# A gated recurrent layer on one core: half B's first memory scan put ahead of half A's second update, and the x products cut into other pieces

## The chip, the cores and the metric

The kernel runs on one core of a Trainium2 chip. The core has a matrix engine (TensorE, PE in the profile; its weight loads are listed apart as PEld), a vector engine (VectorE, DVE), a scalar engine (ScalarE, ACT), a general engine (GpSimd, POOL) and a queue engine (SyncE, SP) that issues DMAs. They run side by side and wait for each other through semaphores. Each of VectorE, ScalarE and GpSimd works through its instructions in the order in which the program lists them. The metric is device time in microseconds of one execution.

## The reference

The layer runs over 512 time steps, for 8 sequences (batch) and 512 hidden units, and its result is added to the input:

```python
def step(h, x_t):
    fused = sigmoid(concatenate([x_t, h]) @ w_W + w_b)
    hidden_state, output_state = split(fused, 2)          # r and z
    memory_state = x_t @ wx_W + wx_b + hidden_state * (h @ wh_W + wh_b)
    h_new = output_state * h + (1.0 - output_state) * tanh(memory_state)
    return h_new
x + all h_new
```

All is in float32. The products with `x_t` depend on nothing that the loop makes; the products with `h` must wait for the previous step's `h_new`.

## The kernel before

**Layout.** The 512 hidden units are four chunks of 128. Chunks 0 and 1 of the state are half A (`hTA`), chunks 2 and 3 half B (`hTB`), each [128 partitions, 8 batch columns, 2 chunks, 3 slots]. A product uses one chunk of state as weights (32 columns) and streams a weight matrix; four of them (j = 0 to 3) write the four 32-partition strips of the output at once. "A group of four" below is such a quadruple.

**One step on TensorE** (line 27, `ORDER`). A0 A1 take the two chunks of `hTA` against 256 columns each, A2 A3 the two chunks of `hTB` against 192 columns each, all into the PSUM tile A; D0 to D3 take all four chunks against 128 columns into tile D; H2 H3 take `hTB` against 64 columns into tile H. Then comes a piece of the products with x for steps to come (line 393), and the next step's A0.

**One step on VectorE** (lines 470 to 495). For half A: transpose `tr` (r gate), transpose into `md1A` (the h product), transpose `tz` (z gate), a one-column memset of the tile `idle`, two memory scans `m` (one for each chunk). Then, for half B: a transpose of a part of A into `md1B` (line 452), `tr` from D, the first update scan of A, the transpose of H into `md1B`, `tz` from D, the second update scan of A, two memory scans, two update scans of B. The memory scan computes r * (h product) + x part, and the update scan z * h + (1 - z) * tanh. ScalarE computes the sigmoids of `tr` (into `md0`) and of `tz` (into `hd0`), the tanh behind each memory scan (into a slot of `hTA` or `hTB`), and a copy of the new state.

The one-column memsets compute nothing. The one at line 441 carries a wait: it waits for VectorE's own transpose into `md1A`, so that the memory scan behind it has to wait for ScalarE's sigmoid alone. For half B the same is reached in another way: the second update of A is made to wait for B's sigmoid (line 481), and the first memory scan of B behind it waits for VectorE's own transpose. Two more memsets stand at the end of every step (line 569).

**Who waits for whom.** A0 needs the first update of A, A1 the second, A2 the first update of B, A3 the second. `tr` of half A needs A3 done, `tr` of half B needs D, the transpose into `md1B` needs H.

**The products with x** (lines 296 to 342). They are made for eight steps (two groups of four steps) at a time, by seven products instead of eight: `x_sum` (GpSimd) and `weight_sum` (VectorE) form sums of x columns and of weights; p1 and p7, p2 and p6, p4 and p3 are run in pairs (j = 0, 1 from the first, j = 2, 3 from the second), and `shared` is added into both banks `xps`. Each k is one half of a contraction. `products` yields after each piece, and the main loop takes one piece per step, from step 4 of eight on. The pieces are 384, 384, 384, 384 columns in steps 4 to 7 of eight, and 288, 96 + 192, 192 + 96, 288 in steps 0 to 3. Around them ScalarE fills the banks with bias (line 534) and copies finished ones to `xs`, VectorE adds the shared differences (lines 508 to 548), and the `x_sum` of the first kind used (number 2) is issued in step 3 of eight (line 539). Nothing is planned by a tool: the order on each engine is the order of the statements.

Of the kernel before, what the change touches and what calls it, by code (L numbers as in the profile page):

```python
# [19 lines left out]


DVE_FILL = 23
IDLE = 3
LAST = 4
SYNC = mybir.DependencyInfo(mybir.DependencyClass.Sync, mybir.DependencyReason.DATA)

# [22 lines left out]
def tile_cond_rnn_residual(  # L49
# [39 lines left out]
    nc = tc.nc  # L89
# [27 lines left out]
    def x_of(c, k, t, n):  # L117

        e, t = divmod(t, TC // 2)
        if c == 0 and e == 0:  # L120
            first = head[:, :NX].rearrange("p (k n) -> p k n", k=NQ)
            return first[:, k, t * B : (t + n) * B]
        return xins[c][:, e, k, t * B : (t + n) * B]
# [19 lines left out]
    def pair(n, name, rows, slots):  # L143

        return const.tile([P, 2, rows, slots], F32, name=name).rearrange("p c n s -> p n c s")
# [24 lines left out]
    for t_ in hd0[0] + hd0[1]:  # L170
        nc.gpsimd.memset(t_[:, :, :, 1], -1.0)
    idle = const.tile([P, IDLE], F32, name="idle")

# [8 lines left out]
    def state(hf, i, slot=2):  # L182

        s = i % GS
        return hT[hf][i % NH][:, B * s : B * s + B, :, slot]
# [8 lines left out]
    def mm(out_, lhsT, rhs, start=False):  # L194
        nc.tensor.matmul(  # L195
            out_, lhsT, rhs, start=start, stop=False, skip_group_check=True
        )
# [27 lines left out]
    def act(key, out_, in_, func, **kw):  # L225
        inst = nc.scalar.activation(out_, in_, func, **kw).ins  # L226
        if key in written:
            tc.declare_no_dep(inst, written[key], reason="ordered through VectorE")
        written[key] = inst
        return inst  # L230

    def seed(g):

        nc.scalar.copy(xps[g % 2][:, COLS], bias[:, COLS])
# [32 lines left out]
    def wx_of(kh, nh):  # L267
        return wx[:, 2 * kh : 2 * kh + 2, 2 * nh : 2 * nh + 2]

    def x_half(o, n, kh):  # L270

        return x_of(o // 2, slice(2 * kh, 2 * kh + 2), 8 * (o % 2) + GS * n, GS)
# [12 lines left out]
    def x_sum(o, n):  # L285

        t_ = [q[o % 2] for q in sx]
        a, b, op = [
            (x_half(o, 1, 0), x_half(o, 1, 1), ALU.add),
            (t_[0], x_half(o, 0, 0), ALU.subtract),  # L290
            (x_half(o, 0, 0), x_half(o, 1, 0), ALU.subtract),
            (x_half(o, 0, 1), t_[1], ALU.subtract),
        ][n]
        nc.gpsimd.tensor_tensor(t_[n], a, b, op)

    def products(o):

        t_ = [q[o % 2] for q in sx]
        p1 = (0, x_half(o, 0, 0), wx_of(0, 0))
        p2 = (0, x_half(o, 0, 1), wx_of(1, 0))  # L300
        p3 = (0, t_[3], wx_of(1, 1))
        p4 = (1, x_half(o, 1, 1), tw[3])
        p6 = (0, t_[1], tw[1])
        p7 = (1, t_[2], tw[2])

        def pair(left, right, k, c0=0, c1=WIDE):
            for j in range(NQ):
                bank, lhs, rhs = left if j < 2 else right
                mm(
                    xps[bank][32 * j : 32 * j + 32, COLS.start + c0 : COLS.start + c1],  # L310
                    lhs[:, k],
                    rhs[:, k, j % 2, c0:c1],
                    start=right is p7 and k == 0 and j >= 2,
                )

        def shared(k):
            for j in range(NQ):
                c0 = HALF * (1 - j // 2)
                mm(
                    xps[j // 2][32 * j : 32 * j + 32, COLS.start : COLS.start + HALF],  # L320
                    t_[0][:, k],
                    tw[0][:, k, j % 2, c0 : c0 + HALF],
                )

        pair(p1, p7, 0)
        yield
        pair(p1, p7, 1)
        yield
        pair(p2, p6, 0)
        yield  # L330
        pair(p2, p6, 1)
        yield
        pair(p4, p3, 0, 0, 288)
        yield
        pair(p4, p3, 0, 288)
        shared(0)
        yield
        shared(1)
        pair(p4, p3, 1, 0, 96)
        yield  # L340
        pair(p4, p3, 1, 96)
        yield

    def take(it, n=None):
        while n is None or n > 0:
# [20 lines left out]
    for i in range(T):  # L366
# [8 lines left out]
        for n in (ORDER if i else FIRST).split():  # L375
# [3 lines left out]
            bank, k = n[0], int(n[1])  # L379
# [17 lines left out]
        def scan(c_, out_, d0, d1):  # L397

            return nc.vector.tensor_tensor_scan(  # L399
                *[t_[:, :, c_].rearrange("p n c s -> p (n c s)") for t_ in (out_, d0, d1)],  # L400
                0.0,
                ALU.mult,
                ALU.add,
            ).ins
# [8 lines left out]
        def turned(n, hf):  # L413
            t_ = work.tile([P, 2, 32], F32, tag=f"t{n}{hf}", name=f"t{n}{hf}_{i}")
            inst = nc.vector.transpose(t_.rearrange("p c n -> p (c n)"), raw[n][hf]).ins  # L415
            return t_[:, :, rows], inst

        r_done = [None, None]
        h_done = [None, None]
# [17 lines left out]

        def turn_z(hf):
            tz, _ = turned("z", hf)
            if hf == 0:  # L440
                inst = nc.vector.memset(idle[:, IDLE - 1 :], 0.0).ins
                tc.add_manual_dep(inst, h_done[0].name, SYNC)
            act(
                ("zc", hf, i % 2),
                hd0[hf][i % 2][:, :, :, 2].rearrange("p n c -> p c n"),
                tz,
                AF.Sigmoid,
                scale=-1.0,
            )
# [9 lines left out]
        def memory(hf, q):  # L459

            c_ = slice(q, q + 1)
            scan(c_, ms[hf], md0[hf][g % 2][:, rows], md1[hf][g % 2][:, rows])
            act(("n", hf, q, i % NH), state(hf, i, 1)[:, :, c_], ms[hf][:, :, c_, 1 + hf], AF.Tanh)

        def update(hf, q):
            s1 = (i + 1) % GS
            new = hT[hf][(i + 1) % NH][:, B * s1 : B * s1 + B]
            return scan(slice(q, q + 1), new, hd0[hf][i % 2], hT[hf][i % NH][:, rows])
# [9 lines left out]
        update(0, 0)  # L478
        turn_h(1)
        turn_z(1)  # L480
        tc.add_manual_dep(update(0, 1), r_done[1].name, SYNC)
        if i == 0:

            seed(2)
        if i == T - 1:
            nc.gpsimd.tensor_tensor(
                ot[:, t, :2, :].rearrange("p c n -> p n c"),
                x_of(c, slice(0, 2), t, 1).rearrange("p c n -> p n c"),
                state(0, T),
                ALU.add,  # L490
            )
        memory(1, 0)
        memory(1, 1)
        update(1, 0)
        update(1, 1)
# [5 lines left out]
        o, u = divmod(i, 2 * GS)  # L501
        nxt, two = o + 1 < NG // 2, o + 2 < NG // 2
# [15 lines left out]
        if u == 0:  # L518
            spread(2 * o + 1, "D")
            if o and nxt:  # L520
                nc.scalar.copy(xps[0][Q01, lo], step_bias[Q01])
                nc.scalar.copy(xps[1][Q23, lo], step_bias[Q23])
        elif u == 1:
            spread(2 * o + 1, "A")
            if o == 0:
                seed(3)
        elif u == 2:
            if o == 0:
                nc.scalar.copy(xs[0][:, SC], xps[0][:, COLS])
            elif nxt:  # L530
                nc.scalar.copy(both[Q23, HALF:], xps[0][Q01, lo])
                nc.vector.tensor_copy(both[Q23, :HALF], xps[1][Q23, lo])
            if two:
                nc.scalar.copy(xps[0][Q01, COLS], bias[Q01, COLS])
        elif u == 3:
            if o == 0:
                nc.scalar.copy(xs[1][:, SC], xps[1][:, COLS])
            if two:
                x_sum(o + 2, 2)
        elif u == 4 and nxt:  # L540
            if o:
                add_(xs[1][Q01, SC], xps[1][Q01, COLS], u3[Q23], ALU.add)
            spread(2 * o + 2, "A")
            if two:
                x_sum(o + 2, 0)
        elif u == 5 and nxt:
            if o:
                add_(xs[1][Q23, SC], u3[Q23], both[Q23], ALU.add)
            if two:
                nc.scalar.copy(xps[0][Q23, COLS], xps[0][Q01, COLS])  # L550
                x_sum(o + 2, 1)
            spread(2 * o + 2, "D")
        elif u == 6 and nxt:
            spread(2 * o + 2, "H")
            if two:
                nc.vector.memset(xps[1][Q01, COLS], 0.0)
                x_sum(o + 2, 3)
        elif u == 7 and nxt:
            if two:
                nc.scalar.copy(u2[Q23], xps[0][Q23, COLS])  # L560
            spread(2 * o + 3, "H")
# [4 lines left out]
        if i == 4:  # L566
            for to, c_ in ((Q01, slice(256, 448)), (Q23, slice(64, 256))):
                nc.vector.tensor_tensor(step_bias[to], bias[Q23, c_], bias[Q01, c_], ALU.subtract)
        for n in range(IDLE - 1):
            nc.vector.memset(idle[:, n : n + 1], 0.0)  # L570
        def add(hf, engine):
            return engine.tensor_tensor(  # L572
# [98 lines left out]
```

## Time and profile before

| | |
|---|---|
| median of 3 runs | 1681.23 us (1681.18 to 1681.54) |
| profiled execution, its own time | 1681.52 us |
| its span in the profile | 1679.7 us |
| TensorE busy | 1667.8 us, 99% |
| VectorE busy | 1402.8 us, 84% |
| ScalarE busy | 1190.5 us, 71% |
| GpSimd busy | 327.2 us, 19% |
| granted TensorE clock | 1.00 |

The span is what lies between the first and the last instruction of the profiled execution. In a row of the timeline stand start, duration, engine, line, operation, the tiles written and read, and how many neighbouring instructions were merged (x16); a bracket gives the idle time before it and who ended it. A row of the groups gives busy time, mean duration in ns, and idle time before it with what ended it. A matmul's record lasts until its result is out and so overlaps the next one's: the distance between starts tells the pace, not the duration. Each float32 product appears as two records.

### The profile page before, as it was taken

How to read it: one execution, taken by the hardware profiler on the slowest of the kernel's cores; microseconds unless marked ns; L12 is line 12 of the kernel's file. 1: busy time of each engine (PE TensorE's matmuls, PEld its weight loads, DVE VectorE, ACT ScalarE, POOL GpSimd, SP SyncE). 2: the span in 40 equal slices, each digit the busy share in tenths (PEclk: the TensorE clock that was granted, in tenths of full speed). 3: DMA queues.
4: the chain of work that ended last, by engine and by line, in shares of the span. 5: the costliest groups of instructions: out<-in, count | busy, mean ns of one | idle time of the engine just before them, and what ended most of it. 6: DMA issues, size and time to landing. Idle time of an engine off the chain costs nothing.

```text
span 1679.7 us, 110201 instructions
## 1 busy us (share of the span) xinstructions
PE 1667.8 (99%) x46078; PEld 1237.3 (74%) x46078; DVE 1402.8 (84%) x10213; ACT 1190.5 (71%) x5884; POOL 327.2 (19%) x1290
## 2 busy tenths in 40 slices
PE   8999999999999999999999999999999999999998
PEld 5777777777777777777777777777777777777776
DVE  6888888888888888888888888888888888888886
ACT  4777777777777777777777777777777777777775
POOL 2221121111211211112112121121121211211211
PEclk9999999999999999999999999999999999999999
DMA  4000000000000000000000000000000000000000
GB/s 178 17 4 17 17 17 17 12 9 17 17 17 17 4 17 17 17 17 4 17 17 17 17 16 5 17 17 17 17 4 17 17 17 17 4 17 11 11 11 10
DMA packets 11452, 30.14 MB, mean 18 GB/s; under 512 B 1220, under 2 KB 1732, under 8 KB 10952
## 3 DMA queue, kind: packets, MB, share of 16 engines
q1 hardware_dynamic: 10800, 22.94, 3.9%
q8 instruction: 360, 5.90, 1.5%
q14 instruction: 140, 1.15, 0.2%
q10 hardware_dynamic: 152, 0.16, 0.0%
HBM read 14.70 MB, written 8.39 MB: 14 GB/s over the span
## 4 chain that ended last, share of the span: by engine, by line
PE 97%; DVE 2%; DMA 1%; ACT 0%; issue 0%
PE A L195 48%; PE D L195 26%; PE xp L195 17%; PE H L195 7%; DMA wd<-in_wd_dram 1%; DVE tr L415 0%; DMA rows<-in_bias_dram 0%; DVE m L399 0%; DVE md1B L452 0%; DVE tw L283 0%; DVE tz L415 0%; DVE md1A L431 0%; DVE hTA L399 0%; DVE hTB L399 0%; ACT hTB L226 0%
## 5 line engine op out<-in xcount | busy, mean ns | idle before, releaser
L195 PE MATMUL A<-wa,hTA 128*32 128x256 f32 x8176 | 535.3, 379 | 3.0 <-DVE hTA L399 3.0
L195 PE MATMUL A<-wa,hTB 128*32 128x192 f32 x8176 | 436.2, 331 | 0.0
L195 PEld LDWEIGHTS A<-wa,hTA 128*32 128x32 f32 x8176 | 255.6, 122 | 233.0 <-DVE hTA L399 171.3
L572 POOL TENSOR_TENSOR ot<-xin,hTB 128x16 f32<-128x16 f32 x503 | 124.8, 248 | 1312.0 <-DVE hTB L399 1301.0
L195 PEld LDWEIGHTS A<-wa,hTB 128*32 128x32 f32 x8176 | 250.8, 123 | 165.8 <-DVE hTB L399 145.4
L195 PE MATMUL D<-wd,hTA 128*32 128x128 f32 x8192 | 317.6, 273 | 1.2 <-DMA wd<-in_wd_dram 1.2
L195 PE MATMUL D<-wd,hTB 128*32 128x128 f32 x8192 | 317.5, 273 | 0.0
L226 ACT ACTIVATE md0A<-tr 128x16 f32<-128x16 f32 x512 | 112.8, 220 | 231.0 <-DVE tr L415 221.6
L195 PEld LDWEIGHTS D<-wd,hTA 128*32 128x32 f32 x8192 | 257.2, 122 | 22.2 <-DMA wd<-in_wd_dram 1.5
L195 PE MATMUL xp<-tw,sx 128*32 128x384 f32 x1984 | 265.3, 406 | 0.0
L415 DVE STREAM_TRANSPOSE tr<-A 128x64 f32<-128x64 f32 x511 | 127.9, 250 | 137.0 <-PE A L195 127.7
L195 PEld LDWEIGHTS D<-wd,hTB 128*32 128x32 f32 x8192 | 240.4, 122 | 0.0
L399 DVE TENSOR_TENSOR_SCAN hTB<-hd0B,hTB 128x24 f32<-128x24 f32 x1024 | 159.9, 198 | 94.4 <-ACT hTB L226 94.4
L195 PE MATMUL H<-wa,hTB 128*32 128x64 f32 x8192 | 208.2, 219 | 0.0
L195 PE MATMUL xp<-wx,xin 128*32 128x384 f32 x1056 | 207.9, 486 | 0.0
L399 DVE TENSOR_TENSOR_SCAN hTA<-hd0A,hTA 128x24 f32<-128x24 f32 x1024 | 194.8, 190 | 0.0
L195 PEld LDWEIGHTS H<-wa,hTB 128*32 128x32 f32 x8192 | 185.5, 122 | 0.0
L226 ACT ACTIVATE hTB<-hTB 128x16 f32<-128x16 f32 x512 | 121.3, 237 | 78.4 <-DVE hTB L399 66.2
L226 ACT ACTIVATE hd0B<-tz 128x16 f32<-128x16 f32 x512 | 115.7, 226 | 74.9 <-DVE tz L415 27.6
L226 ACT ACTIVATE hTB<-m 128x8 f32<-128x8 f32 x1024 | 163.8, 208 | 4.4
L226 ACT ACTIVATE hTA<-m 128x8 f32<-128x8 f32 x1024 | 160.5, 206 | 2.2
L399 DVE TENSOR_TENSOR_SCAN m<-md0A,md1A 128x16 f32<-128x16 f32 x1024 | 142.2, 181 | 8.8
(103 smaller groups left out, 2586.2 us busy)
## 6 DMA issues: line engine op xcount, KB each, us to landing
xin<-in_x_dram SPq DMA_DIRECT2D x31, 256.0 KB, 3.5
out_dram<-ot SPq DMA_DIRECT2D x31, 256.0 KB, 2.1
wx<-in_wx_dram SPq DMA_DIRECT2D x4, 768.0 KB, 6.8
wa<-in_wa_dram SPq DMA_DIRECT2D x4, 512.0 KB, 9.6
wd<-in_wd_dram SPq DMA_DIRECT2D x1, 768.0 KB
wd<-in_wd_dram SPq DMA_DIRECT2D x1, 256.0 KB, 11.2
out_dram<-ot SPq DMA_DIRECT2D x1, 192.0 KB, 1.9
head<-in_xh_dram ACTq DMA_DIRECT2D x1, 144.0 KB, 4.8
```

Source lines behind the costliest of these rows:

```text
L195: nc.tensor.matmul(out_, lhsT, rhs, start=start, stop=False, skip_group_check=True)
L226: inst = nc.scalar.activation(out_, in_, func, **kw).ins
L399: return nc.vector.tensor_tensor_scan(*[t_[:, :, c_].rearrange("p n c s -> p (n c s)") for t_ in (out_, d0, d1)], 0.0, ALU.mult, ALU.add,).ins
L415: inst = nc.vector.transpose(t_.rearrange("p c n -> p (c n)"), raw[n][hf]).ins
L572: return engine.tensor_tensor(ot[:, t, 2 * hf : 2 * hf + 2, :].rearrange("p c n -> p n c"), x_of(c, slice(2 * hf, 2 * hf + 2), t, 1).rearr ...
```

## The change

Three things are changed together. On VectorE the first memory scan of half B comes ahead of the second update of half A; that update no longer waits for B's sigmoid, and half B gets a one-column memset of its own that waits for the transpose of H, as half A has. The pieces of the x products become 128 (only for the first of eight steps of a later set; it is taken at the end of the step before), 256 + 64, 320, 384, 384, 320, 64 + 192 + 64, 192 + 128, 192 columns, so that six steps of eight have 320 and two have 384. Since the first piece of the next set now runs at the end of step 3 of eight, its `x_sum` is issued in step 2, and the start flag is set only on the piece that begins at column 0. The number of one-column memsets at the end of a step stays two; `seed(2)` of the first step moves by one statement.

```diff
--- before.py
+++ after.py
@@ -20,7 +20,7 @@
 
 
 DVE_FILL = 23
-IDLE = 3
+IDLE = 4
 LAST = 4
 SYNC = mybir.DependencyInfo(mybir.DependencyClass.Sync, mybir.DependencyReason.DATA)
 
@@ -310,7 +310,7 @@
                     xps[bank][32 * j : 32 * j + 32, COLS.start + c0 : COLS.start + c1],
                     lhs[:, k],
                     rhs[:, k, j % 2, c0:c1],
-                    start=right is p7 and k == 0 and j >= 2,
+                    start=right is p7 and k == 0 and c0 == 0 and j >= 2,
                 )
 
         def shared(k):
@@ -322,24 +322,28 @@
                     tw[0][:, k, j % 2, c0 : c0 + HALF],
                 )
 
-        pair(p1, p7, 0)
+        pair(p1, p7, 0, 0, 128)
+        if o > 2:
+            yield
+        pair(p1, p7, 0, 128)
+        pair(p1, p7, 1, 0, 64)
         yield
-        pair(p1, p7, 1)
+        pair(p1, p7, 1, 64)
         yield
         pair(p2, p6, 0)
         yield
         pair(p2, p6, 1)
         yield
-        pair(p4, p3, 0, 0, 288)
+        pair(p4, p3, 0, 0, 320)
         yield
-        pair(p4, p3, 0, 288)
+        pair(p4, p3, 0, 320)
         shared(0)
+        pair(p4, p3, 1, 0, 64)
         yield
         shared(1)
-        pair(p4, p3, 1, 0, 96)
+        pair(p4, p3, 1, 64, 192)
         yield
-        pair(p4, p3, 1, 96)
-        yield
+        pair(p4, p3, 1, 192)
 
     def take(it, n=None):
         while n is None or n > 0:
@@ -437,9 +441,8 @@
 
         def turn_z(hf):
             tz, _ = turned("z", hf)
-            if hf == 0:
-                inst = nc.vector.memset(idle[:, IDLE - 1 :], 0.0).ins
-                tc.add_manual_dep(inst, h_done[0].name, SYNC)
+            inst = nc.vector.memset(idle[:, IDLE - 2 + hf : IDLE - 1 + hf], 0.0).ins
+            tc.add_manual_dep(inst, h_done[hf].name, SYNC)
             act(
                 ("zc", hf, i % 2),
                 hd0[hf][i % 2][:, :, :, 2].rearrange("p n c -> p c n"),
@@ -478,10 +481,11 @@
         update(0, 0)
         turn_h(1)
         turn_z(1)
-        tc.add_manual_dep(update(0, 1), r_done[1].name, SYNC)
         if i == 0:
 
             seed(2)
+        memory(1, 0)
+        update(0, 1)
         if i == T - 1:
             nc.gpsimd.tensor_tensor(
                 ot[:, t, :2, :].rearrange("p c n -> p n c"),
@@ -489,7 +493,6 @@
                 state(0, T),
                 ALU.add,
             )
-        memory(1, 0)
         memory(1, 1)
         update(1, 0)
         update(1, 1)
@@ -532,10 +535,11 @@
                 nc.vector.tensor_copy(both[Q23, :HALF], xps[1][Q23, lo])
             if two:
                 nc.scalar.copy(xps[0][Q01, COLS], bias[Q01, COLS])
+                if o:
+                    x_sum(o + 2, 2)
         elif u == 3:
             if o == 0:
                 nc.scalar.copy(xs[1][:, SC], xps[1][:, COLS])
-            if two:
                 x_sum(o + 2, 2)
         elif u == 4 and nxt:
             if o:
@@ -566,7 +570,7 @@
         if i == 4:
             for to, c_ in ((Q01, slice(256, 448)), (Q23, slice(64, 256))):
                 nc.vector.tensor_tensor(step_bias[to], bias[Q23, c_], bias[Q01, c_], ALU.subtract)
-        for n in range(IDLE - 1):
+        for n in range(IDLE - 2):
             nc.vector.memset(idle[:, n : n + 1], 0.0)
         def add(hf, engine):
             return engine.tensor_tensor(
```

## The prediction

> **What bounds the kernel now.** I read the page first (busy shares, clock, chain), then the timeline of TensorE over one period of eight steps, then VectorE, ScalarE and the weight loads around one handover. Step number modulo eight is called u; the step that starts at 796.96 is u = 0.
>
> ```profile
> span 1679.7 us, 110201 instructions
> PE 1667.8 (99%) x46078; PEld 1237.3 (74%) x46078; DVE 1402.8 (84%) x10213; ACT 1190.5 (71%) x5884; POOL 327.2 (19%) x1290
> PEclk9999999999999999999999999999999999999999
> PE 97%; DVE 2%; DMA 1%; ACT 0%; issue 0%
> L195 PEld LDWEIGHTS A<-wa,hTB 128*32 128x32 f32 x8176 | 250.8, 123 | 165.8 <-DVE hTB L399 145.4
> ```
>
> TensorE looks full at full clock. But a matmul's record is long and overlaps the next, so a short stall does not show as idle time; the weight loads do show one, 145.4 us of waiting for `hTB`. Starts are safer than busy time:
>
> ```profile
> 796.96 1.05 PE L195 MATMUL A<-wa,hTA 128*32 128x256 f32 x16
> 797.82 0.83 PE L195 MATMUL A<-wa,hTB 128*32 128x192 f32 x16
> 798.47 0.62 PE L195 MATMUL D<-wd,hTA 128*32 128x128 f32 x16
> ...
> 800.05 1.05 PE L195 MATMUL A<-wa,hTA 128*32 128x256 f32 x16
> ...
> 803.26 1.05 PE L195 MATMUL A<-wa,hTA 128*32 128x256 f32 x16
> 804.19 0.87 PE L195 MATMUL A<-wa,hTB 128*32 128x192 f32 x16
> 804.88 0.62 PE L195 MATMUL D<-wd,hTA 128*32 128x128 f32 x16
> ...
> 805.76 0.41 PE L195 MATMUL H<-wa,hTB 128*32 128x64 f32 x16
> ...
> 806.47 1.05 PE L195 MATMUL A<-wa,hTA 128*32 128x256 f32 x16
> ...
> 809.68 1.05 PE L195 MATMUL A<-wa,hTA 128*32 128x256 f32 x16
> ...
> 813.05 1.05 PE L195 MATMUL A<-wa,hTA 128*32 128x256 f32 x16
> ...
> 822.81 1.05 PE L195 MATMUL A<-wa,hTA 128*32 128x256 f32 x16
> ```
>
> Eight steps take 822.81 - 796.96 = 25.85 us. The last three (384 columns of x products each) take 9.76, so 3.255 each. The step at 796.96 (288 columns) takes 3.09. The other 288-column steps take 3.21, and the one at 809.68 (384) takes 3.37. In the clean step the second half of A starts 0.86 after the first and D 0.65 after that; in the step at 803.26 these are 0.93 and 0.69. So 0.07 + 0.04 = 0.11 us is lost where A2 waits for `hTB`, in four steps of eight (u = 1 to 4, each following a 288-column step). Without it the period would be 4 x 3.095 + 4 x 3.255 = 25.40: 0.45 us lost per period, and over 62 periods (512 steps are 64, of which the first and the last differ) 28 us.
>
> What makes `hTB` late is a run of work on VectorE and ScalarE:
>
> ```profile
> 803.06 0.25 DVE L431 STREAM_TRANSPOSE md1B<-H 128x64 f32<-128x64 f32 x1
> 803.21 0.21 DVE L415 STREAM_TRANSPOSE tz<-D 128x64 f32<-128x64 f32 x1
> 803.34 0.21 DVE L399 TENSOR_TENSOR_SCAN hTA<-hd0A,hTA 128x24 f32<-128x24 f32 x1
> 803.47 0.28 DVE L399 TENSOR_TENSOR_SCAN m<-md0B,md1B 128x24 f32<-128x24 f32 x2
> 803.93 0.31 DVE L399 TENSOR_TENSOR_SCAN hTB<-hd0B,hTB 128x24 f32<-128x24 f32 x2 [0.18 <-ACT hTB L226]
> 804.30 0.07 DVE L570 MEMSET idle<- 128x1 f32 x2
> ```
>
> ```profile
> 803.09 0.22 ACT L226 ACTIVATE md0B<-tr 128x16 f32<-128x16 f32 x1
> 803.68 0.32 ACT L226 ACTIVATE hTB<-m 128x8 f32<-128x8 f32 x2
> ```
>
> ```profile
> 803.60 0.23 PEld L195 LDWEIGHTS A<-wa,hTA 128*32 128x32 f32 x8 [0.20 <-DVE hTA L399]
> 804.19 0.51 PEld L195 LDWEIGHTS A<-wa,hTB 128*32 128x32 f32 x16 [0.35 <-DVE hTB L399]
> ```
>
> The second update of A starts at 803.34, 0.03 after ScalarE's sigmoid for B ends (803.31). B's first memory scan comes behind it at 803.47, the tanh 0.21 after that scan's start, the `hTB` scans 0.25 after the tanh's. A1's weight load starts 0.05 after the update of A ends (803.55 to 803.60); A2's, at 804.19, so puts the end of the first `hTB` scan at 804.14, and the matmuls behind it run 0.04 longer than unstalled ones. This run starts from the previous step's A3, so a loop of 3.21 us through VectorE bounds the steps that are not bounded by TensorE.
>
> **The change, part by part.** *Balance.* The same 2688 columns of x products are spread as 320 in six steps and 384 in two (u = 6, 7). One column costs (3.255 - 3.095) / 96 = 1.67 ns, so a 320-column step has a floor of 3.255 - 0.107 = 3.148. There are 13 groups of four matmuls for 10. A pass of 256 columns lasts 0.216 (three spacings in 1.05 less one record of 0.40) and one of 64 lasts 0.056, so a pass has a fixed 3 ns and the three added groups cost 0.02 per period. Floor: 6 x 3.148 + 2 x 3.255 + 0.02 = 25.42, which is 27 us less over 62 periods.
>
> *Scan order.* On VectorE the order after `tz` of B becomes: memset (new, waits for the transpose of H), B's first memory scan, A's second update, B's second memory scan. The sigmoid's wait moves from the update to that memory scan. Two things follow. B's first scan starts earlier than 803.47, so A2's operand is earlier. And A's second update, which A1's weights wait for, moves from 803.34 to behind that scan. Behind the new wait in VectorE's queue stand all of these, and for them wait the tanh, A1 and A2.
>
> When does B's scan start? No row shows this order, so I bound it. Not before the transpose of H has ended (803.31) and been handed on (0.03, as from ScalarE to VectorE at 803.34) and the memset has gone (0.01, the spacing of the two memsets at 804.30): 803.35. The latest by half A, which has this very order:
>
> ```profile
> 805.31 0.21 DVE L431 STREAM_TRANSPOSE md1A<-A 128x64 f32<-128x64 f32 x1
> 805.44 0.21 DVE L415 STREAM_TRANSPOSE tz<-A 128x64 f32<-128x64 f32 x1
> 805.60 0.06 DVE L441 MEMSET idle<- 128x1 f32 x1
> 805.67 0.28 DVE L399 TENSOR_TENSOR_SCAN m<-md0A,md1A 128x16 f32<-128x16 f32 x2
> ```
>
> ```profile
> 805.42 0.22 ACT L226 ACTIVATE md0A<-tr 128x16 f32<-128x16 f32 x1 [0.52 <-DVE tr L415]
> ```
>
> There the memset is 0.08 after the transpose's end and the scan 0.07 later: 803.31 + 0.15 = 803.46. But in half A the scan's 0.07 is ended by the sigmoid (805.64, plus 0.03), which in half B is done long before. I take the memset 0.16 behind `tz` as in half A (803.37) and the scan 0.01 behind it: 803.38. That a memset itself holds up nothing is shown early in the run, where the transposition that follows two of them starts with them:
>
> ```profile
> 41.85 0.23 DVE L415 STREAM_TRANSPOSE tr<-A 128x64 f32<-128x64 f32 x1
> 41.85 0.07 DVE L570 MEMSET idle<- 128x1 f32 x2
> ```
>
> [...]
>
> In u = 4 to 7 the transpose of H lasts longer, and nothing holds the update there:
>
> ```profile
> 815.98 0.30 DVE L431 STREAM_TRANSPOSE md1B<-H 128x64 f32<-128x64 f32 x1
> 816.12 0.20 DVE L415 STREAM_TRANSPOSE tz<-D 128x64 f32<-128x64 f32 x1
> 816.26 0.18 DVE L399 TENSOR_TENSOR_SCAN hTA<-hd0A,hTA 128x24 f32<-128x24 f32 x1
> 816.35 0.28 DVE L399 TENSOR_TENSOR_SCAN m<-md0B,md1B 128x24 f32<-128x24 f32 x2
> ```
>
> From 803.38: A's second update starts 0.10 later (one scan follows another by 0.09 at 816.35, and two that take 0.18 each take 0.28), 803.48; it ends 0.18 later, 803.66; its weight load starts 0.05 later, 803.71; the matmul counts from 0.04 later, 803.75. A1 could have started at 803.26 + 0.43 = 803.69 with 288 columns and at 803.75 with 320. A2 follows A1 by 0.43: 804.18, against 804.23 now (804.19 + 0.04). The loop goes from 3.21 to 3.16, and it is now A1, not A2, that ends it: B's own path would allow 804.14. So a step of 320 columns takes 3.16, just over its floor.
>
> Two steps do worse. In u = 4 and 5 the transpose of H ends at 816.28; 0.04 more puts the scan at 816.32, only 0.03 before its 816.35, where u = 2 gains 0.09 (803.47 to 803.38). So the loop is 0.06 longer there: 3.22. In u = 6 and 7 that hides under 3.26. Sum: 4 x 3.16 + 2 x 3.22 + 2 x 3.26 = 25.60; with 0.02 for the tail of VectorE's work in u = 1 and 4 (B's second scan and second update come later, and the copies behind them with it) 25.62. That is 0.23 less than 25.85; times 62, 14.3 us.
>
> *The rest* costs nothing as long as its cover holds. The 128 columns of the next products at the end of u = 3 need the bias copy and one sum earlier:
>
> ```profile
> 808.09 0.48 ACT L534 COPY xp<-bias 64x384 f32<-64x384 f32 x1
> 807.93 0.32 POOL L294 TENSOR_TENSOR sx<-xin 128x64 f32<-128x64 f32 x1
> ```
>
> The copy ends at 808.57. The x products follow H's four passes, at 805.76 + 4 x 0.056 = 805.98, in u = 3 one step of 3.21 later, 809.19, and the new ones are the second part of these: 0.6 and more of cover. The sum moves one step ahead on GpSimd, 81% idle, whose next work waits for `hTB` anyway. If the cover were gone, a sum's 0.32 us once in eight steps would be 20 us. SP's queue is untouched: no DMA moves. The second memset per step is the one already counted.
>
> The profiled execution took 1681.5 us by its own time (span 1679.7), 0.3 above the median 1681.2; 1681.2 - 14.3 = 1667.
>
> **The rivals.** (1) *Slower: the new memset holds the scan as in half A.* With 0.07 from memset to scan B's scan starts at 803.44, A2 is at 804.24 and the loop 3.22; in u = 4 to 7 the scan starts at 816.39, 0.04 later than now, so 0.13 worse than the 803.38 case: 3.29. 4 x 3.22 + 4 x 3.29 = 26.04, or +12 us, 1693; at the outer bounds (803.46, 816.43) 4 x 3.24 + 4 x 3.33 = 26.28, +27 us, 1708. The price is A1's wait in every step. It decides once the scan starts later than 803.42. For it: the 0.07 row. Against: that row's wait has another end.
> (2) *TensorE's floor.* The scan at 803.35 and a short transpose everywhere: 25.42 and 1654. Against it: the 0.30 row.
> (3) *The balance alone works.* The moved scan gains B nothing that A1 does not take back, the loop stays 3.20 to 3.21: 6 x 3.205 + 2 x 3.255 = 25.74, less 7 us, 1674. That is the change doing half of what it does.
> (4) *No change*: the scan at 803.42, loop 3.20, u = 4 to 7 3.26: 25.84, 1681.
>
> **How the numbers follow.** A difference of 0.2%, 3.4 us, is about what a measurement can tell from none. My forecast (1660 to 1671) has 0.34, the floor 0.16, the balance alone 0.14, no change 0.09, slower 0.27. So faster 0.64, same 0.09, slower 0.27. The range takes in the floor and of the slower case the half below its 1693: 1654 to 1691; the likeliest case alone is 1660 to 1671.
>
> **What would show it.** Starts of A in the 320-column steps 3.15 to 3.18 apart, and 3.22 in u = 4 and 5; the weight-load wait of A for `hTB` gone or small, and one for `hTA` in its place; on VectorE the memory scan of B some 0.17 behind `tz` and the update of A 0.10 behind it. A gap of 0.23 from `tz` to that scan would be rival 1. Wrong would also be a longer wait of the x products for ScalarE or GpSimd in u = 3, or a later transposition of A in u = 1 and 4.

## The result, and the profile after

The changed kernel takes 1669.17 us (median of 4 runs, 1668.88 to 1669.37) beside 1681.38 (1681.18 to 1681.67) for the kernel before on the same chip: 12.2 us less, a ratio of 0.9927 (95% interval 0.9910 to 0.9944). It is faster by 0.7%, and the interval does not reach 1. The forecast was 1667, with a range of 1654 to 1691. The profiled execution took 1668.88 with a span of 1667.1, 12.6 less than the span before.

The page of the changed kernel: span, busy shares, and the two groups of weight loads that wait (busy time, mean ns, then idle time before them and who ended it).

```profile
span 1667.1 us, 113659 instructions
PE 1655.4 (99%) x47566; PEld 1256.4 (75%) x47566; DVE 1463.3 (88%) x10725; ACT 1206.6 (72%) x5884; POOL 328.6 (20%) x1290
L195 PEld LDWEIGHTS A<-wa,hTA 128*32 128x32 f32 x8176 | 225.4, 124 | 227.4 <-DVE hTA L403 217.4
L195 PEld LDWEIGHTS A<-wa,hTB 128*32 128x32 f32 x8176 | 264.8, 122 | 120.5 <-DVE hTB L403 94.5
```

The line for `hTA` in the kernel before:

```profile
L195 PEld LDWEIGHTS A<-wa,hTA 128*32 128x32 f32 x8176 | 255.6, 122 | 233.0 <-DVE hTA L399 171.3
```

VectorE has the 512 added memsets (10213 to 10725). The wait for `hTB` fell from 145.4 to 94.5 us, and the one for `hTA` rose from 171.3 to 217.4. These totals give only the direction, for loads waited for both halves before and after; which of the waits stall TensorE is read from the starts. TensorE's timeline over one period (the first column is the start): A0 of some steps, and A2 or D where they are used.

```profile
509.40 1.05 PE L195 MATMUL A<-wa,hTA 128*32 128x256 f32 x16
510.26 0.83 PE L195 MATMUL A<-wa,hTB 128*32 128x192 f32 x16
...
512.55 1.05 PE L195 MATMUL A<-wa,hTA 128*32 128x256 f32 x16
...
515.72 1.09 PE L195 MATMUL A<-wa,hTA 128*32 128x256 f32 x16
516.63 0.83 PE L195 MATMUL A<-wa,hTB 128*32 128x192 f32 x16
517.28 0.62 PE L195 MATMUL D<-wd,hTA 128*32 128x128 f32 x16
...
518.92 1.05 PE L195 MATMUL A<-wa,hTA 128*32 128x256 f32 x16
...
525.27 1.12 PE L195 MATMUL A<-wa,hTA 128*32 128x256 f32 x16
526.21 0.83 PE L195 MATMUL A<-wa,hTB 128*32 128x192 f32 x16
...
535.04 1.04 PE L195 MATMUL A<-wa,hTA 128*32 128x256 f32 x16
```

The step at 509.40 is u = 0. Eight steps take 535.04 - 509.40 = 25.64 us. From A0 to A2 it is 0.86 in the unstalled u = 0, but 0.91 at 515.72 and 0.94 at 525.27: A1, between them, now waits. From A2 to D it is 0.65 at 516.63, as in the clean step before: A2 waits no more. The stall has gone from A2 to A1, and is smaller. It is so over the whole run: from A2's first pass to D the median is now 0.650 in all eight steps, where it was 0.689 in four of them; A1's second pass came 0.216 after its first in every step before, and comes up to 0.255 after it now.

VectorE's timeline around the handover that ends at 516.63, and the weight loads there:

```profile
515.50 0.25 DVE L435 STREAM_TRANSPOSE md1B<-H 128x64 f32<-128x64 f32 x1
515.65 0.21 DVE L419 STREAM_TRANSPOSE tz<-D 128x64 f32<-128x64 f32 x1
515.80 0.20 DVE L403 TENSOR_TENSOR_SCAN m<-md0B,md1B 128x24 f32<-128x24 f32 x1
515.82 0.06 DVE L444 MEMSET idle<- 128x1 f32 x1
515.92 0.18 DVE L403 TENSOR_TENSOR_SCAN hTA<-hd0A,hTA 128x24 f32<-128x24 f32 x1
516.02 0.18 DVE L403 TENSOR_TENSOR_SCAN m<-md0B,md1B 128x24 f32<-128x24 f32 x1
```

```profile
516.15 0.19 PEld L195 LDWEIGHTS A<-wa,hTA 128*32 128x32 f32 x8 [0.30 <-DVE hTA L403]
516.55 0.55 PEld L195 LDWEIGHTS A<-wa,hTB 128*32 128x32 f32 x16 [0.20 <-DVE hTB L403]
```

The transpose of H ends at 515.75, and B's scan starts 0.05 later (median 0.043). Half A's update stands 0.12 behind, ends at 516.10, and A1's weight load comes 0.05 after it.

Worked out from all starts of the two traces: the median distance from the second pass of A2 in step u to that in the next step, over 58 periods, in us.

| step u | 0 | 1 | 2 | 3 | 4 | 5 | 6 | 7 | sum |
|---|---|---|---|---|---|---|---|---|---|
| before | 3.213 | 3.213 | 3.210 | 3.207 | 3.255 | 3.255 | 3.255 | 3.255 | 25.863 |
| forecast (0.02 for the tail apart) | 3.16 | 3.16 | 3.16 | 3.16 | 3.22 | 3.22 | 3.26 | 3.26 | 25.62 |
| after | 3.155 | 3.199 | 3.153 | 3.189 | 3.220 | 3.235 | 3.255 | 3.255 | 25.661 |

The difference of 0.20 times 62 periods is 12.5 us, which is the gain.

The forecast's last test was the transposition of A in u = 1 and 4. It does come later: 0.79 after the second pass of A2 instead of 0.74 (medians 0.788 and 0.794, 0.738 in the other steps). The tail of VectorE's work that does it, in u = 1:

```profile
513.51 0.56 DVE L516 TENSOR_TENSOR u<-xp,u 64x384 f32<-64x384 f32 x1
514.11 0.21 DVE L265 STREAM_TRANSPOSE md1A<-xs 128x32 f32<-128x32 f32 x1
514.27 0.07 DVE L574 MEMSET idle<- 128x1 f32 x2
514.37 0.25 DVE L419 STREAM_TRANSPOSE tr<-A 128x64 f32<-128x64 f32 x1
```

No bracket stands at `tr`: in the steps in which it waits for TensorE it comes at 0.738, so A was ready by then, and VectorE did not come to it. It starts 0.03 after the memsets' records end (514.34).

### The profile page after: what moved, and what is told of

Its sections match the earlier page's. It is cut to its first block, busy times and chain, and to the rows that moved or that the text cites. A ratio compares the mean times of both kernels' runs of the same rounds, so it can differ in the third digit from the quotient of the medians.

```text
span 1667.1 us, 113659 instructions
## 1 busy us (share of the span) xinstructions
PE 1655.4 (99%) x47566; PEld 1256.4 (75%) x47566; DVE 1463.3 (88%) x10725; ACT 1206.6 (72%) x5884; POOL 328.6 (20%) x1290
## 4 chain that ended last, share of the span: by engine, by line
PE 97%; DVE 2%; DMA 1%; ACT 0%; issue 0%; SPq 0%; DVEq 0%
PE A L195 47%; PE D L195 26%; PE xp L195 17%; PE H L195 7%; DMA wd<-in_wd_dram 1%; DVE tr L419 0%; DVE m L403 0%; DMA head<-in_xh_dram 0%; DVE md1B L455 0%; DVE tz L419 0%; DVE tw L283 0%; DVE md1A L435 0%; DVE hTB L403 0%; DVE hTA L403 0%; ACT hTB L226 0%
## 5 line engine op out<-in xcount | busy, mean ns | idle before, releaser
L195 PE MATMUL A<-wa,hTA 128*32 128x256 f32 x8176 | 550.7, 384 | 3.1 <-DVE hTA L403 3.0
L195 PE MATMUL A<-wa,hTB 128*32 128x192 f32 x8176 | 426.0, 326 | 0.0
L195 PEld LDWEIGHTS A<-wa,hTA 128*32 128x32 f32 x8176 | 225.4, 124 | 227.4 <-DVE hTA L403 217.4
L195 PEld LDWEIGHTS A<-wa,hTB 128*32 128x32 f32 x8176 | 264.8, 122 | 120.5 <-DVE hTB L403 94.5
L195 PE MATMUL xp<-tw,sx 128*32 128x192 f32 (+5 forms) x2480 | 276.2, 358 | 0.0
L403 DVE TENSOR_TENSOR_SCAN hTB<-hd0B,hTB 128x24 f32<-128x24 f32 x1024 | 206.8, 208 | 44.3 <-ACT hTB L226 0.4
L195 PE MATMUL xp<-wx,xin 128*32 128x384 f32 (+4 forms) x1552 | 218.7, 384 | 0.0
L226 ACT ACTIVATE hTB<-m 128x8 f32<-128x8 f32 x1024 | 211.4, 216 | 0.0
L403 DVE TENSOR_TENSOR_SCAN m<-md0B,md1B 128x24 f32<-128x24 f32 x1024 | 196.6, 192 | 0.0
L403 DVE TENSOR_TENSOR_SCAN hTA<-hd0A,hTA 128x24 f32<-128x24 f32 x1024 | 188.6, 184 | 0.0
```

Of the source, the lines that this page charges most:

```text
L195: nc.tensor.matmul(out_, lhsT, rhs, start=start, stop=False, skip_group_check=True)
L403: return nc.vector.tensor_tensor_scan(*[t_[:, :, c_].rearrange("p n c s -> p (n c s)") for t_ in (out_, d0, d1)], 0.0, ALU.mult, ALU.add,).ins
```

## Experiments

Theory: the gain is the earlier scan of B, ended by A1's wait for half A's second update; what is missing to the forecast is VectorE's tail in u = 1 and 4. Rivals: the balance does most of it; the memset costs its scan something; the held start of one scan in u = 5 is more than the tail. Runs 1 to 4 shared a chip and a kernel before at 1681.77 us, 5 to 8 one at 1681.24, 9 to 11 one at 1681.43. The diffs show the main lines, without those that only fit the width of `idle`; two memsets stay at the end of a step where nothing else is said.

**1. The pieces alone** (VectorE's order as before).

```diff
-            inst = nc.vector.memset(idle[:, IDLE - 2 + hf : IDLE - 1 + hf], 0.0).ins
-            tc.add_manual_dep(inst, h_done[hf].name, SYNC)
+            if hf == 0:
+                inst = nc.vector.memset(idle[:, IDLE - 1 :], 0.0).ins
+                tc.add_manual_dep(inst, h_done[0].name, SYNC)
...
+        tc.add_manual_dep(update(0, 1), r_done[1].name, SYNC)
-        memory(1, 0)
-        update(0, 1)
...
+        memory(1, 0)
```

> The new pieces of 320 and 384 columns with VectorE's old order. If the wait of A2 for the first hTB scan is a loop of 3.20 to 3.21 us that the columns do not change, six steps take 3.205 and two 3.255: 25.74 a period, some 7 us less than before, 1674. If the pieces alone made the gain, it comes out at 1669 as the changed kernel does; if they do nothing, at 1681.

1676.31 us, ratio 0.9967 (0.9954 to 0.9979): 5.5 us, not quite half of the 12.2 of both; the rival's 1674 was close. The weight loads at one handover:

```profile
517.36 0.63 PEld L195 LDWEIGHTS A<-wa,hTA 128*32 128x32 f32 x16
518.29 0.51 PEld L195 LDWEIGHTS A<-wa,hTB 128*32 128x32 f32 x16 [0.30 <-DVE hTB L403]
```

A1's loads run on without a wait and A2's waits, as before. The steps of 320 columns take 3.203 to 3.217 from A0 to A0 (medians), and only u = 0, which follows a 384-column step, reaches 3.148. The loop of 3.21 goes through VectorE's old order, and the pieces do not touch it.

**2. The order alone** (the pieces as before): the hunks of the diff in `turn_z` and in the step's order, without those in `products` and around `x_sum`.

> VectorE's new order with the old pieces of 288 and 384 columns. If the new order shortens the loop to about 3.16 to 3.20 and A1 now ends it, the four 288-column steps take that instead of 3.21 and the four of 384 stay at 3.255: about 25.72, 8 to 9 us less, 1672 to 1673, with waits for hTA in place of those for hTB. If the order helps only where 320 columns cover A1, it comes out at 1681 or above.

1672.40 us, ratio 0.9943 (0.9929 to 0.9958): 9.4 us. The wait has moved to A1:

```profile
513.83 0.19 PEld L195 LDWEIGHTS A<-wa,hTA 128*32 128x32 f32 x8 [0.30 <-DVE hTA L399]
514.22 0.55 PEld L195 LDWEIGHTS A<-wa,hTB 128*32 128x32 f32 x16 [0.20 <-DVE hTB L399]
```

So the order is the larger part. 5.5 and 9.4 are 14.8 alone and 12.2 together: the two are not independent. By the loops of the table, what is missing lies in u = 5, which takes 3.215 with the pieces alone and 3.235 with both, and in u = 3, 3.171 with the order alone and 3.189 with both. So in u = 5, where the transpose of H is long, the new order costs 0.02 instead of gaining.

**3. Without half B's memset.** The scan itself then has to wait both for ScalarE's sigmoid and for VectorE's own transpose of H.

```diff
-            inst = nc.vector.memset(idle[:, IDLE - 2 + hf : IDLE - 1 + hf], 0.0).ins
-            tc.add_manual_dep(inst, h_done[hf].name, SYNC)
+            if hf == 0:
+                inst = nc.vector.memset(idle[:, IDLE - 2 : IDLE - 1], 0.0).ins
+                tc.add_manual_dep(inst, h_done[0].name, SYNC)
```

> The changed kernel without half B's memset; B's first memory scan then waits both for VectorE's transpose and for ScalarE's sigmoid. If the memset is free and only carries a wait, the scan cannot come earlier, and with the two waits it comes up to 0.04 later: 1669 to 1684. If the memset takes a slot of its own (0.06 us), the scan comes that much earlier and six steps gain: TensorE's floor, near 1655.

1699.32 us, ratio 1.0103 (1.0088 to 1.0118): 30 us slower than the changed kernel, twice the worst that was expected for it. The page and VectorE's timeline:

```profile
span 1697.4 us, 113657 instructions
PE 1683.6 (99%) x47566; PEld 1248.1 (74%) x47566; DVE 1488.3 (88%) x10213; ACT 1232.5 (73%) x5884; POOL 327.7 (19%) x1290
```

```profile
517.99 0.25 DVE L435 STREAM_TRANSPOSE md1B<-H 128x64 f32<-128x64 f32 x1
518.14 0.21 DVE L419 STREAM_TRANSPOSE tz<-D 128x64 f32<-128x64 f32 x1
518.34 0.21 DVE L403 TENSOR_TENSOR_SCAN m<-md0B,md1B 128x24 f32<-128x24 f32 x1
```

512 memsets are gone from VectorE, yet the program is only 2 instructions shorter: 510 instructions that the page does not count as busy have taken their place. The trace has them on VectorE, at the line of the scans: 513 semaphore instructions instead of 3, about one per step, for the scan's second wait. The transpose ends at 518.24 and the scan starts 0.10 later instead of 0.05 (medians 0.103 and 0.043). The loops of u = 0 to 5 are 0.06 to 0.08 longer (means), those of u = 6 and 7, which 384 columns cover, by 0.015 at most: 0.46 per period, or 29 of the 30 us. The memset is what keeps the new order from costing time.

**4. Two more memsets in half B,** behind the one that waits.

```diff
             tc.add_manual_dep(inst, h_done[hf].name, SYNC)
+            if hf:
+                nc.vector.memset(idle[:, 4:5], 0.0)
+                nc.vector.memset(idle[:, 5:6], 0.0)
```

> The changed kernel with three memsets in half B in place of one; only the first has a wait. If a one-column memset costs nothing to what stands behind it, or 0.01 us, the time stays at 1669 to 1676. If each costs the 0.06 us that it is recorded with, two more cost 0.12 in every step's A1 loop: six steps of some 3.30 and two of 3.33, about 1710 to 1720.

1677.05 us, ratio 0.9971 (0.9959 to 0.9983): 7.5 us less gained than with one. Over 2 x 512 memsets that is 7 ns for each, if the whole difference is theirs, with u = 6 and 7 counted, whose loops stay at 3.255.

```profile
517.64 0.25 DVE L435 STREAM_TRANSPOSE md1B<-H 128x64 f32<-128x64 f32 x1
...
517.95 0.20 DVE L403 TENSOR_TENSOR_SCAN m<-md0B,md1B 128x24 f32<-128x24 f32 x1
517.96 0.06 DVE L444 MEMSET idle<- 128x1 f32 x1
...
517.97 0.06 DVE L448 MEMSET idle<- 128x1 f32 x1
```

The scan starts 0.06 after the transpose's end (517.89) instead of 0.05. The medians are 0.060 and 0.043, so two more memsets put it off by 0.017, 8 to 9 ns each; the loops of u = 0 to 5 are 0.018 to 0.025 longer. A memset's record lasts 0.06, but the records lie on top of one another and of the scan's. If each cost what its record lasts, two more would, as an estimate, have cost 0.12 per step; the 0.017 measured decides against that for memsets of one column.

**5. A read that lifts the hold in u = 5.** A hold means here that an instruction starts only 0.02 to 0.04 after all before it on VectorE have ended, with no wait for another engine that accounts for it. In u = 5 half A's first memory scan starts 0.03 later than in u = 0 (medians 1.305 and 1.275 after A2's second pass): 0.041 after the end of the memset before it instead of 0.010, and 0.061 after the end of its sigmoid instead of 0.033, though the sigmoid starts at 1.022 in both. The last instruction before it that read from SBUF is an addition whose SBUF input begins at partition 64; the three transposes between them read PSUM, from partition 0 on. The edit adds a one-column copy whose input begins at partition 0. If the addition's read is the cause, the copy takes the lateness on itself: 0.03 once in a period is, as an estimate, 2 us, so near 1667.

```diff
+        if u == 4 and o and nxt:
+            nc.vector.tensor_copy(idle[:, 4:5], zeros[:, :1])
```

> The changed kernel with a one-column copy (SBUF, partition 0 on, to SBUF) at the end of VectorE's work once in eight steps, behind the addition whose inputs start at partition 64. In the step after it half A's first memory scan starts 0.03 later than in other steps. [...] If the 0.03 has another cause the time stays at 1669 or is longer by a hidden instruction's nothing.

1667.98 us, ratio 0.9921 (0.9906 to 0.9936), 1.45 less than the changed kernel beside it. That is under 0.1%, but all four times (1667.77 to 1668.11) lie below the four of the changed kernel (1669.35 to 1669.65), and the loop of u = 5 went from 3.235 to 3.205. In the changed kernel and then in this one, half A in u = 5:

```profile
527.11 0.25 DVE L419 STREAM_TRANSPOSE tr<-A 128x64 f32<-128x64 f32 x1
...
527.57 0.06 DVE L444 MEMSET idle<- 128x1 f32 x1
527.67 0.28 DVE L403 TENSOR_TENSOR_SCAN m<-md0A,md1A 128x16 f32<-128x16 f32 x2
```

```profile
526.72 0.15 DVE L576 COPY idle<-zeros 128x1 f32<-128x1 f32 x1
526.83 0.25 DVE L419 STREAM_TRANSPOSE tr<-A 128x64 f32<-128x64 f32 x1
...
527.30 0.06 DVE L444 MEMSET idle<- 128x1 f32 x1
527.37 0.28 DVE L403 TENSOR_TENSOR_SCAN m<-md0A,md1A 128x16 f32<-128x16 f32 x2
```

0.56 from `tr` to the scan has become 0.54, and the median of the scan 1.276. Held, the scan came 0.04 after the end of the memset before it (527.57 + 0.06 = 527.63); with the copy it comes 0.01 after that (527.30 + 0.06 = 527.36). So the scan was held where the last read of SBUF began at partition 64, and that cost 0.03 in the loop of u = 5. What makes such a read hold it, and whether other partitions do, was not shown.

**6. The small transposes ahead of the long additions,** one step later than in the changed kernel. The tail of u = 1 and 4 keeps as many instructions; only their order changes.

```diff
-            turn_x(1, 0)
+        ahead = 2 * o + (1 if u < 4 else 2)
+        if ahead < NG:
+            turn_x(ahead, u % GS)
...
-        ahead = 2 * o + (1 if u < 3 else 2 if u < 7 else 3)
-        if ahead < NG:
-            turn_x(ahead, (u + 1) % GS)
```

> The changed kernel with the small transposes of the x part issued one step later each, ahead of the long additions instead of behind them. In the changed kernel half A's first transpose is 0.05 late in two steps of eight, behind addition, small transpose and memsets. If that tail is what makes it late, the two steps have it at its usual 0.74 after A2's second pass; but the addition is then the last to read SBUF, from partition 64 on, and the first memory scan of half A is held 0.03 as in the two steps where that stands now. Net 0.02 in two steps: 2 to 3 us, 1666 to 1667. If TensorE is what the transpose waits for, nothing changes: 1669.

1687.93 us, ratio 1.0041 (1.0026 to 1.0056): slower than the kernel before. A miss. `tr` in u = 1 and 4 came only 0.03 and 0.02 earlier (medians 0.758, 0.771), and a new wait arose elsewhere. The tail of u = 7, the changed kernel first, on VectorE and then on ScalarE:

```profile
510.17 0.52 DVE L514 COPY xs<-xp 64x384 f32<-64x384 f32 x1
...
511.17 0.25 DVE L419 STREAM_TRANSPOSE tr<-A 128x64 f32<-128x64 f32 x1 [0.33 <-PE A L195]
```

```profile
510.79 0.47 ACT L564 COPY u<-xp 64x384 f32<-64x384 f32 x1 [0.26 <-DVE xs L514]
```

The same in this kernel:

```profile
516.82 0.20 DVE L265 STREAM_TRANSPOSE md1B<-xs 128x32 f32<-128x32 f32 x1
517.12 0.55 DVE L516 COPY xs<-xp 64x384 f32<-64x384 f32 x1
...
517.78 0.25 DVE L419 STREAM_TRANSPOSE tr<-A 128x64 f32<-128x64 f32 x1
```

```profile
517.76 0.47 ACT L563 COPY u<-xp 64x384 f32<-64x384 f32 x1 [0.59 <-DVE idle L573]
```

ScalarE's copy waits for VectorE's long copy: it starts 0.10 and 0.09 after that copy's end (510.69 and 517.67), though the second bracket names the memsets behind it. A short copy and the next sigmoid stand behind it in ScalarE's queue. The copy ends at 518.23, 0.45 after `tr` has started; in the changed kernel at 511.26, 0.09 after it. Half A's memory scan in u = 0 so comes 1.573 after A2's second pass instead of 1.275, and the loop of u = 0 takes 3.444 instead of 3.155. That is 0.29 of the 0.31 that a period got longer.

**7. The same with one-column copies behind the three long additions,** to lift the hold of `tr` as well: run 6, with the edit of run 5 made for `u in (0, 3, 4)`.

> The same with the one-column copy behind each of the three long additions that are followed by slack. Both causes gone: u = 1 from 3.20 to TensorE's 3.155, the loops of u = 4 and 5 shorter by 0.05 and 0.03: 0.12 less a period, 7 us, near 1662. If the long additions were not what delays these steps: 1669; if the copies hold the transpose up themselves, above 1669.

1701.45 us, ratio 1.0122 (1.0105 to 1.0139). A miss too. The copy itself starts only 0.02 after the memsets behind the addition have ended (523.91 + 0.07 = 523.98), lasts 0.15, and `tr` comes behind its end:

```profile
523.91 0.07 DVE L573 MEMSET idle<- 128x1 f32 x2
524.00 0.15 DVE L575 COPY idle<-zeros 128x1 f32<-128x1 f32 x1
524.18 0.25 DVE L419 STREAM_TRANSPOSE tr<-A 128x64 f32<-128x64 f32 x1
```

524.00 + 0.15 = 524.15, and `tr` 0.03 later. Its median is 0.926 in u = 1 and 0.937 in u = 4, later by 0.14 than in the changed kernel. The long loop of u = 0 from run 6 is in this time too (3.446). A copy helped only where something else covers it, as in run 5, where `tr` waits for TensorE.

**8. The changed kernel again,** beside runs 5 to 7.

> The changed kernel again, beside the other three on the same chip: 1669, 0.9927 of before.

1669.43 us, ratio 0.9930 (0.9915 to 0.9945).

**9. Without the two memsets at the end of a step.**

```diff
-        for n in range(IDLE - 2):
-            nc.vector.memset(idle[:, n : n + 1], 0.0)
```

> The changed kernel without the two one-column memsets at the end of every step. In two steps of eight half A's first transpose starts 0.03 after the end of the second of them, and it is 0.05 late there. If it is held until every earlier instruction has finished, it now starts 0.03 after the small transpose's end, 0.02 earlier in two steps: 2 to 3 us less, 1666 to 1667. If VectorE's tail as such does not set these steps, 1669.

1666.98 us, ratio 0.9914 (0.9897 to 0.9930), some 2.3 less than the changed kernel. The tail of u = 1:

```profile
513.30 0.22 DVE L265 STREAM_TRANSPOSE md1A<-xs 128x32 f32<-128x32 f32 x1
513.55 0.25 DVE L419 STREAM_TRANSPOSE tr<-A 128x64 f32<-128x64 f32 x1
```

`tr` again starts 0.03 after what stands ahead of it has ended (513.52), and so came earlier by what the memsets took of the tail: 0.771 and 0.772. The loops of u = 1 and 4 went from 3.199 and 3.220 to 3.188 and 3.191. So the length of VectorE's tail is part of what bounds these two steps. It is 0.04 per period for both, against 0.03 for the hold of run 5.

**10. The tail emptied in another way.** The small transposes of steps 0 and 3 go to other steps, where VectorE waits for TensorE (`tr` at 0.738); the long additions stay where they are. With the copy of run 5.

```diff
-            turn_x(ahead, (u + 1) % GS)
+            for e in {1: (1, 2), 2: (3,), 4: (0,), 5: (1,), 6: (2, 3), 7: (0,)}.get(u, ()):
+                turn_x(ahead, e)
...
+        if u == 4 and o and nxt:
+            nc.vector.tensor_copy(idle[:, 4:5], zeros[:, :1])
```

> The changed kernel with the one-column copy of the run before (step 4 of eight) and with the small transposes of steps 0 and 3 of eight moved into steps 1, 5 and 6, so that in those two steps nothing stands behind the long addition. Half A's first transpose should be on time in u = 1 and 4 (0.74 after A2's second pass, 0.05 earlier), while its first memory scan is held 0.03 there. Net 0.02 to 0.03 in two steps beside the copy's 1.5 us: 1665 to 1666. If the late transpose is not the cost of these steps, 1668.

1662.12 us (1661.32 to 1664.36), ratio 0.9887 (0.9872 to 0.9902): 7 less than the changed kernel, better than expected. VectorE in u = 1:

```profile
511.40 0.56 DVE L516 TENSOR_TENSOR u<-xp,u 64x384 f32<-64x384 f32 x1
...
512.20 0.25 DVE L419 STREAM_TRANSPOSE tr<-A 128x64 f32<-128x64 f32 x1
...
512.77 0.28 DVE L403 TENSOR_TENSOR_SCAN m<-md0A,md1A 128x16 f32<-128x16 f32 x2
```

`tr` is at 0.738 or 0.739 in all eight steps. The loops of the table above are 3.152, 3.181, 3.155, 3.184, 3.192, 3.157, 3.255, 3.255, in sum 25.53. The emptied tail is the smaller part of this. In u = 1 and 4 the scan now comes 0.57 after `tr`, 0.04 after the memset before it (512.67 + 0.06), as if held behind the long addition, which was expected. It stands at 1.306 (medians), no earlier than the 1.304 and 1.306 of run 9: the two loops gain 0.05 together on the changed kernel, and in run 9 they had gained 0.04. The loop of u = 5 gains 0.078 of the 0.13 per period. The copy gave 0.030 of it in run 5; the rest goes with the transpose of H, which now lasts 0.247 (median) instead of 0.297 and was not expected to change. In u = 6 and 7 it still lasts 0.303. What makes it long is not settled.

**11. Run 10 without the memsets at the end of a step.**

> The same without the two memsets at the end of every step. If nothing is late in these steps any more, the memsets are free and it comes out as the run before, 1665 to 1666; if the transpose is still held by them, up to 2 us less.

1661.47 us (1661.22 to 1665.13), ratio 0.9886 (0.9871 to 0.9901): no difference from run 10. With the tail short enough the memsets lie under the wait for TensorE.

## Why the prediction was right, and where its sizes were off

- **The stall's place.** Right: A2 waits no more, and A1 is the end of the loop. Runs 1 and 2 show that this comes from the order and not from the pieces. The sign in the weight loads came only in part: the wait for `hTB` fell by a third and is not small, since most of it stalls nothing.
- **When B's scan starts.** The prediction put it 0.17 behind `tz`; it is 0.15 (515.65 to 515.80), and in all eight steps 0.043 after the end of the transpose of H (medians). That is the 0.04 that the prediction gave as its earliest bound and used for u = 4 and 5; for the other steps it took 0.07 (803.38), so there the scan came 0.03 earlier than forecast. Rival 1, in which the memset holds the scan by 0.07, falls: run 4 prices a memset at 8 to 9 ns, which is the prediction's 0.01 and not the nothing that it read at 41.85.
- **The update behind it.** 0.10 was predicted, 0.12 recorded. The scan came 0.03 earlier and the update 0.02 farther behind it, so the errors nearly cancel for A1, which is luck. In all steps the second memory scan follows the update by 0.10. The loops of u = 0 and 2, where nothing else interferes, are 3.155 and 3.153 for a predicted 3.16.
- **The long transpose of H.** 3.22 was right in u = 5 (3.235, with the hold of run 5 in it). In u = 4 the 3.22 came out for another reason, by luck: there the transpose of H lasted only 0.262, and a late `tr` made the step long. The pieces bear on that length: with the old ones and the new order (run 2) it is 0.302 in u = 4 and 0.251 in u = 3, with the new ones (run 1) 0.270 in both.
- **The tail of VectorE in u = 1 and 4. This is the term that was mis-sized:** the prediction gave it 0.02 per period, and `tr` came 0.05 late in both steps, 0.106 in all. In the loop of u = 1 that is 0.04. The reason is visible in the medians of u = 0: relative to A2's second pass B's first update went from 2.748 to 2.650, by 0.10, but the second one only from 2.873 to 2.847, by 0.03, since its memory scan stands behind half A's update, while the step itself became 0.06 shorter. The long addition, next behind it in the tail, so starts 0.05 later as seen from the next A2 (0.07 before its second pass instead of 0.12), in u = 4 too, and what follows had no slack. Runs 9 and 10 shorten the tail, and `tr` comes earlier, but they get back only 0.01 to 0.02 of the 0.04 in u = 1: the scan of half A stays at 1.304 to 1.306, where it is 1.275 in u = 0. In run 10 that looks like the hold of run 5, here behind the long addition of u = 0 and 3; no run takes that addition out of the tail.
- **Not foreseen:** u = 3 takes 3.189. There half A's memory scan comes 0.015 later (its sigmoid is 0.012 late on ScalarE), and the transpose of H lasts 0.273 instead of 0.246 in u = 2.
- **The sum.** Against the forecast u = 1 lost 0.04, u = 3 0.03 and u = 5 0.015; the 0.02 set aside for the tail and roundings of 0.02 come off: 25.66 for 25.62. Times 62 that is 2.5 us, and the time is 2.2 above the forecast.
- **The other rivals.** The balance alone is worth 5.5 us (run 1), so the third falls. The floor of 25.42 was not reached: A1's waits, 0.24 per period, are just the difference to 25.66.
- **The rest** was free as predicted: the x products of u = 3, 192 + 128 columns, start 0.056 after H's last pass and take 0.543, as those of u = 2 and 4, which have 320 columns too.

## What to carry to other kernels

When two operands that are wanted one after the other come out of the same engine, put the chain with the longer way still to go first (here worth 9.4 us, run 2), and look for the end of the loop at the other one. A shorter loop also has to be met by what follows in the engine's queue: list the steps in which the tail after the critical work already ends just in time, for there the gain is lost (here 0.04 of it in u = 1). Try an idle instruction that carries a wait for the one behind it: here it was worth 30 us.

## What the runs showed of the hardware that was not expected

- A one-column memset is recorded as 0.06 us, but puts off what follows it by 8 to 9 ns (run 4), and its recorded start can lie behind that of the instruction after it (515.82 and 515.80).
- B's first scan starts 0.103 after the end of the transpose of H when it has to wait for two others itself, and 0.043 after it when a memset carries the first wait (medians): 30 us over the run (run 3).
- On VectorE the scan of u = 5, which reads SBUF from partition 0 on where the last read of SBUF began at partition 64, began 0.041 after the end of the memset before it (median); run 5 shows it by taking the cause away. The starts of others fit it: the small transposes begin 0.032 and 0.035 after the end of the long additions of u = 0 and 3, which read and write SBUF from partition 64 on, but 0.076 before the end of the long copy of u = 7, which reads PSUM from partition 0 on (medians of 62 each, changed kernel), and `tr` in u = 1 and 4, which reads PSUM from partition 0 on where those additions read it from partition 64 on, begins 0.03 after the end of what stands ahead of it (run 9). A one-column copy in that position lasts 0.15 (runs 5 and 7), where a one-column memset is recorded as 0.06.
- The transpose of H lasts 0.25 in some steps and 0.30 in others, with the same shape; the pieces of the x products change it in u = 3 and 4 (runs 1 and 2), and moving other transposes changed it in u = 5 (run 10). Why stays open.
